# Recommender forward pass: 401 instead of 132 gathered tiles fetched row by row, other rings and buffers, and a reordered end

## The chip, the cores and the metric

The kernel runs on one core of a Trainium2 chip. The metric is the device time in microseconds (us) of one execution, the lower the better. Profiles show one execution; its span is the time from its first to its last instruction. The engines are named as in the profile: PE (TensorE, with PEld for its weight loads), DVE (VectorE), ACT (ScalarE), POOL (GpSimd) and SP (SyncE). PEq, ACTq, POOLq and SPq are their queues of instructions, in which DMAs are issued.

## The reference

The reference scores 16,384 samples. Each has 69 user fields and one label, all of them row numbers of one table `emb` of 100,001 rows with 96 numbers (384 bytes). Cut to what matters:

```python
u  = emb[batch_user]                      # 16384 x 69 x 96
ql = emb[batch_label[:, 0]]               # 16384 x 96
z  = concat([q, u, q - u, q * u])         # q is ql, once for each field
h  = dice(z @ W1 + b1, a1)                # 64 numbers
att = (h @ W2 + b2) @ W3 + b3             # one number for each field
pre = where(batch_user < ITEM_NUM, u * att, 0)
pooled = einsum('gf,bfe->bge', window, pre)     # 69 fields into 10 groups
x  = concat([pooled, ql])
h  = dice(bn(x @ Wf1 + bf1), af1)         # 200 numbers
h  = dice(bn(h @ Wf2 + bf2), af2)         # 80 numbers
return h @ Wf3 + bf3                      # one score for each sample
```

`dice(x)` is `(alpha * (1 - p) + p) * x` with a sigmoid `p` of `x`. In bytes, nearly all of the work is the fetching of 16,384 x 69 rows.

## The kernel before

The samples are cut into 32 blocks (`NBLK`) of 512. A **chunk** is one field of one block: 512 rows, in four tiles of 128 rows. There are 32 x 69 = 2208 chunks, and the main loop takes them in 1104 **pairs**, one pair in a step.

**Fetching.** `fetch(i)` (L354) fills one buffer of `upool` with the pair's eight tiles. For each tile POOL issues one indirect DMA (`gather`, L255, the instruction at L256), which fetches 128 rows by 128 row numbers in SBUF. PE turns each tile (`transpose`, recorded at L318) into `ptr`, features on partitions. DVE copies `ptr` to `uT` (L369) and multiplies it with the label's rows to `quT` (L370). The labels' own rows come by four gathers for each block (`head_gather`, L322). `upool` has 14 buffers, so POOL can be up to 14 pairs ahead of PE.

**Single rows.** The last tile (`SLOT` 3) of some chunks is not gathered. Its 128 rows are fetched by 128 direct DMAs of 384 bytes, issued by SP or ACT (`class Singles`, L268). For 32 rows at a time the queue reads 32 offsets from SBUF into registers (L279), and then it issues one DMA for each row (L294). The tile lands in a buffer of a ring (`ring`), four buffers for each of the two engines; PE waits on a semaphore for all 128 rows (`wait_for_single`, L311). SP issues a tile for one chunk in 17 steps (`SP_STEPS`), 64 in all, each a whole tile at once, placed in its queue 24 steps ahead of its use. ACT issues 8 rows in each step (`ACT_ROWS`), a tile in 16 steps, 68 in all; its rows stand between its activations, the first four ahead of the step's sigmoid and the others behind it in groups of three (`busy`, L506).

**Attention.** `hidden(i)` (L372) makes the hidden layer `ph` of a pair on PE (L377, L379), and ACT its sigmoid `y` (L381). `gate` (L384) is an activation on ACT (L386) and a product on DVE (L387). `attend` (L389) has one more matmul for each chunk (`pa`, L394), and DVE multiplies it with `uT` to `pre` (L396).

**Top.** `top1` (L398) adds the chunk's share of the 200 numbers to two sums `p` in PSUM (L407), in two halves of 100; a chunk is two matmuls in the code and four in the trace, as each of them runs as two passes. The last field closes the block: `top1_gates`, `top2`, `top3` and `store` make its scores.

**The order** is written out by hand: `plan` is a list of work for each step, filled by `at(step, ...)`, and every engine runs its instructions in this order. In step i of the main part stand the gate of pair i-3, `attend` of pair i-4, the hidden layer of pair i-2, `top1` of pair i-5 and the fetch of pair i. So a result of ACT is used a step after it was made. The last `CLOSE` = 6 steps (L551 to L579) have shorter distances: the hidden layer of the last pair, its `attend` and `top1`, and the whole top of the last block come after the last gather. In them ACT issues no rows. The functions of the change follow.

Of the kernel before, what the change touches and what calls it, by code (L numbers as in the profile page):

```python
# [18 lines left out]
P = 128  # L19
# [17 lines left out]

NUT, NQUT = 12, 8

CLOSE = 6  # L40

NV = 4
PER_BANK = 512 // F

ROW_BYTES = 4 * E
SLOT = 3
SP_STEPS = 17
SP_FIRST = 8
SP_AHEAD = 24
SP_CHUNKS = [2 * (int(SP_STEPS * s) + SP_FIRST) + 1 for s in range(64)]  # L50
SP_RING = 4
ACT_ROWS = 8
ACT_FIRST = 4
ACT_GROUP = 3
ACT_AHEAD = 5
ACT_CHUNKS = [2 * ((s + 1) * P // ACT_ROWS + ACT_AHEAD) for s in range(68)]
ACT_RING = 4
SINGLES = SP_CHUNKS + ACT_CHUNKS
NSB = (len(SINGLES) + P - 1) // P
NSEM = 4  # L60
RING_BYTES = 4096


# [51 lines left out]
def rec_kernel(  # L115
# [15 lines left out]

    const = ctx.enter_context(tc.tile_pool(name="const", bufs=1))
    ipool = ctx.enter_context(tc.tile_pool(name="ipool", bufs=2))
    upool = ctx.enter_context(tc.tile_pool(name="upool", bufs=14))
    ypool = ctx.enter_context(tc.tile_pool(name="ypool", bufs=4))
    ppool = ctx.enter_context(tc.tile_pool(name="ppool", bufs=6))
    bpool = ctx.enter_context(tc.tile_pool(name="bpool", bufs=2))
# [125 lines left out]
    def call(f, *args):  # L263
        return lambda: f(*args)
# [43 lines left out]
    def single(c, t):  # L308
        return places.get(c) if t == SLOT else None
# [41 lines left out]
            if k < m  # L351
        ]

    def fetch(i, between=None):  # L354

        u = upool.tile([P, 8, E], F32, tag="u", name=f"u{i}")
        for j in range(2):
            if j == 1 and between:
                between()
            c = 2 * i + j  # L360
            n, k = chunk_of(c)
            ptr = ps_tr.tile([E, BLK], F32, tag="tr", name=f"ptr{c}")
            for t in range(NQ):
                if single(c, t):
                    wait_for_single(c, t)
                else:
                    gather(rows, u[:, 4 * j + t, :], ids[n][:, 4 * k + t : 4 * k + t + 1])
                read_rows(nc.tensor.transpose, ptr[:, t * P : (t + 1) * P], u, c, t, ident)
            nc.vector.tensor_copy(uTs[c % NUT][0:E], ptr)  # L369
            nc.vector.tensor_tensor(quTs[c % NQUT][0:E], ptr, qTs[n % 2][0:E], ALU.mult)  # L370
# [27 lines left out]
    def top1(c):  # L398
# [6 lines left out]
        pre = pres.pop(c)  # L405
        for h, p in enumerate(p1s[n]):
            nc.tensor.matmul(p, V[:, k, h * DH : (h + 1) * DH], pre, start=False, stop=(k == F - 1))  # L407

    def top1_gates(n):

# [43 lines left out]
        nc.vector.tensor_copy(r, p4)  # L454
        nc.sync.dma_start(out=out[n0 * P : n1 * P].rearrange("(m p) o -> m (p o)", p=P), in_=r)

    def top3_last(n):
        x2 = x2s.pop(n)
        p3 = ps_x.tile([1, BLK], F32, tag="x", name="p3_last")
        nc.tensor.matmul(p3, wf3, x2, start=True, stop=True)  # L460
        r = ypool.tile([P, BLK], F32, tag="y", name="r_last")[0:1]
        nc.vector.tensor_scalar(r, p3, bf3c[0:1], None, ALU.add)
        nc.sync.dma_start(out=out[n * BLK :].rearrange("p o -> o p"), in_=r)

    pres, p1s, x1s, x2s, qs, phs, ys = ({} for _ in range(7))
# [3 lines left out]
    def at(step, *work):  # L469
        plan.setdefault(step, []).extend(work)  # L470
# [81 lines left out]
    tops(c, late + both(c - 5))  # L552
    at(c, call(attends, c - 3))
    tops(c, both(c - 4))
    at(c, call(fetch, c, call(hide, c - 1)))
    at(c + 1, call(attends, c - 2))
    tops(c + 1, both(c - 3))
    at(c + 1, call(attends, c - 1))
    tops(c + 1, both(c - 2))
    at(c + 1, call(fetch, c + 1, call(hide, c)))  # L560
    for i in range(c + 2, NPAIR):
        tops(i, both(i - 3))
        at(i, call(attends, i - 2), call(fetch, i, call(hide, i - 1)))
    i = NPAIR
    tops(i, both(i - 3))
    at(i, call(hide, last), call(attends, i - 2))
    tops(i, both(i - 2))
    at(i, call(store, 0, (NBLK - 1) * NQ), call(attends, last))
    tops(i, both(last))

    def finish():
        n = NBLK - 1
        for job in top1_gates(n):
            job()
        for job in top2(n):
            job()
        top3_last(n)

    at(i, finish)  # L579

    for n in range(NBLK):
        first = n * F // 2
# [86 lines left out]
```

## Time and profile before

| | |
|---|---|
| runs of the kernel before | 11,058.13, 11,061.62, 11,063.75 us (median 11,061.62) |
| the profiled execution: its own time | 11,063.24 us |
| its span | 11,061.5 us |
| PE busy | 9580.9 us, 87% of the span |
| POOL busy | 8332.4 us, 75% |
| DVE busy | 5087.8 us, 46% |
| ACT busy | 2055.4 us, 19% |
| mean clock granted to PE | 0.929 of full speed |
| moved by DMA | 456.87 MB, 41 GB/s |

A share of busy time alone does not tell the bound: PE's share grows where its clock is low, and the time in which ACT and SP issue DMAs is not counted as busy. In the rows of the groups, the numbers behind the bar are the busy time in us and the mean of one instruction in ns, then the idle time ahead of these instructions and what ended it. In a row of waits stand the sum in us, the number of times and the longest. A row of the timeline has its start and length in us, the engine, the line, and after x the number of instructions merged; in brackets the idle time before it. A row for one tile or line has the shortest, the median and the longest duration in ns, and the first and last start in us.

### The profile page before, as it was taken

What the parts mean: (1) busy time and instruction counts of PE and PEld (TensorE: products, weight loads), DVE (VectorE), ACT (ScalarE), POOL (GpSimd) and SP (SyncE); (2) the same over time, 40 slices, a digit from 0 to 9 for tenths busy, and PEclk for the clock granted to TensorE, in tenths of its full rate; (3) what the DMA queues carried; (4) which work ended last, traced back from release to release, by engine and by line L of the source; (5) the groups of instructions that cost most, each with busy time, mean ns of one, the idle gap of its engine ahead of it and who ended that gap; (6) DMA issues with size and microseconds to landing.
All of it is one profiled execution on the core that took longest, in us unless ns stands there. A gap on an engine that the chain in (4) does not pass through costs nothing.

```text
span 11061.5 us, 125036 instructions
## 1 busy us (share of the span) xinstructions
PE 9580.9 (87%) x32079; PEld 3517.5 (32%) x32079; DVE 5087.8 (46%) x7995; ACT 2055.4 (19%) x3058; POOL 8332.4 (75%) x8834
## 2 busy tenths in 40 slices
PE   8888888888888888888888888888888888888888
PEld 4333333333333333333333333333333333333333
DVE  4444444444444444444444444444444444444444
ACT  2211111111111111111111111111111111111111
POOL 7777777777777777777777777777777777777776
PEclk8999999999999999999999999999999999999999
DMA  2222222222222222222222222222222222222221
GB/s 55 41 42 42 41 41 41 43 41 41 41 41 43 41 41 41 41 43 41 41 41 41 43 41 41 41 41 43 41 41 41 41 43 41 41 41 41 40 40 35
DMA packets 319007, 456.87 MB, mean 41 GB/s; under 512 B 175253, under 2 KB 175889, under 8 KB 318162
## 3 DMA queue, kind: packets, MB, share of 16 engines
q0 software_dynamic: 282496, 434.48, 19.8%
q1 hardware_dynamic: 18386, 11.02, 0.4%
q10 hardware_dynamic: 17408, 3.38, 0.2%
q8 instruction: 259, 4.24, 0.2%
q14 instruction: 458, 3.75, 0.1%
HBM read 448.18 MB, written 0.07 MB: 41 GB/s over the span
## 4 chain that ended last, share of the span: by engine, by line
POOL 44%; PE 24%; issue 21%; DMA 10%; DVE 1%; ACT 0%; POOLq 0%; ACTq 0%; DVEq 0%
POOL u L256 43%; PE p L407 10%; DMA u<-in_rows,ids 10%; PE ph L377 4%; PE pa L394 4%; PE ph L379 3%; PE ptr L318 2%; POOL q L256 1%; PE pV L250 0%; PE p L404 0%; PE p L429 0%; DVE quT L370 0%; DMA q<-in_emb,ids 0%; DVE uT L369 0%; ACT g L437 0%
## 5 line engine op out<-in xcount | busy, mean ns | idle before, releaser
L256 POOL DMA_INDIRECT u<-in_rows,ids x8700 | 8210.8, 944 | 2652.6 <-issue 2481.3
L407 PE MATMUL p<-pre,V 96*100 96x512 f32 x8832 | 4077.9, 604 | 2.3 <-DVE pre L396 2.3
L369 DVE COPY uT<-ptr 96x512 f32<-96x512 f32 x2208 | 1512.1, 685 | 5307.5 <-PE ptr L318 5296.3
L318 PE MATMUL ptr<-ident,u 128*96 128x128 f32 x8700 | 1583.9, 286 | 1407.0 <-DMA u<-in_rows,ids 1380.6
L407 PEld LDWEIGHTS p<-pre,V 96*100 96x100 f32 x8832 | 1399.5, 168 | 2751.3 <-issue 2747.1
L381 ACT ACTIVATE y<-ph 128x512 f32<-128x512 f32 x1104 | 659.1, 597 | 7997.0 <-PE ph L379 7996.3
L318 PEld LDWEIGHTS ptr<-ident,u 128*96 128x96 f32 x8700 | 1030.2, 127 | 2461.4 <-DMA u<-in_rows,ids 1798.2
L396 DVE SCALAR_TENSOR_TENSOR pre<-pa,bb,uT 96x512 f32<-96x512 f32 x2208 | 1544.7, 738 | 43.1 <-PE pa L394 32.9
L394 PE MATMUL pa<-y,vrep 64*96 64x512 f32 x4416 | 1514.2, 723 | 43.8 <-DVE cT L342 18.4
L370 DVE TENSOR_TENSOR quT<-ptr,qT 96x512 f32<-96x512 f32 x2208 | 1492.9, 676 | 0.0
L377 PE MATMUL ph<-uT,AW 128*64 128x512 f32 x4416 | 1449.0, 737 | 0.9 <-ACT uT L349 0.9
L379 PE MATMUL ph<-quT,BW 128*64 128x512 f32 x4416 | 1291.1, 664 | 0.0
L386 ACT ACTIVATE y<-y,wn,na1c 128x512 f32<-128x512 f32 x1104 | 897.5, 813 | 604.2 <-ACT y L381 590.1
L387 DVE TENSOR_TENSOR y<-ph,y 128x512 f32<-128x512 f32 x1104 | 747.5, 677 | 22.7 <-ACT y L386 21.7
L379 PEld LDWEIGHTS ph<-quT,BW 128*64 128x64 f32 x4416 | 366.7, 159 | 816.2 <-issue 813.9
L377 PEld LDWEIGHTS ph<-uT,AW 128*64 128x64 f32 x4416 | 247.6, 153 | 1046.3 <-issue 998.5
L394 PEld LDWEIGHTS pa<-y,vrep 64*96 64x96 f32 x4416 | 324.5, 173 | 310.9 <-issue 90.4
L349 ACT COPY uT<-cT 32x512 f32<-32x512 f32 x384 | 230.1, 611 | 69.3 <-issue 50.6
L438 DVE SCALAR_TENSOR_TENSOR x<-p,wf,g 80x512 f32<-80x512 f32 x32 | 23.9, 746 | 304.1 <-ACT g L437 304.1
L349 ACT COPY quT<-cT 32x512 f32<-32x512 f32 x256 | 155.7, 608 | 1.1 <-DVE cT L342 1.1
L256 POOL DMA_INDIRECT q<-in_emb,ids x128 | 121.0, 945 | 40.7 <-issue 38.7
L420 DVE SCALAR_TENSOR_TENSOR x<-p,wf,g 100x512 f32<-100x512 f32 x64 | 46.6, 751 | 137.2 <-ACT g L419 137.2
(60 smaller groups left out, 731.5 us busy)
## 6 DMA issues: line engine op xcount, KB each, us to landing
ring<-in_rows ACTq DMA_DIRECT2D x8704, 0.4 KB
u<-in_rows,ids POOLq DMA_INDIRECT x8700
ring<-in_rows SPq DMA_DIRECT2D x8192, 0.4 KB
ids<-in_idx SPq DMA_DIRECT2D x8, 560.0 KB, 3.8
wv<-in_fields SPq DMA_DIRECT2D x1, 2434.5 KB, 12.1
q<-in_emb,ids POOLq DMA_INDIRECT x128
wn<-in_near SPq DMA_DIRECT2D x1, 226.0 KB, 3.2
wf<-in_far SPq DMA_DIRECT2D x1, 184.0 KB, 3.2
```

The costliest lines, as they stand in the source:

```text
L256: nc.gpsimd.indirect_dma_start(out=dst, out_offset=None, in_=table, in_offset=bass.IndirectOffsetOnAxis(ap=index, axis=0),)
L318: ins = op(out, ring[:, at[0]].bitcast(F32) if at else u[:, 4 * (c % 2) + t, :], other, **how)
L369: nc.vector.tensor_copy(uTs[c % NUT][0:E], ptr)
L370: nc.vector.tensor_tensor(quTs[c % NQUT][0:E], ptr, qTs[n % 2][0:E], ALU.mult)
L377: nc.tensor.matmul(p, AW, uTs[c % NUT], start=True, stop=False)
L379: nc.tensor.matmul(p, BW, quTs[c % NQUT], start=False, stop=True)
L381: nc.scalar.activation(y, ph, AF.Sigmoid, scale=S_DICE)
L386: nc.scalar.activation(ys[i], ys[i], AF.Identity, bias=a1c, scale=na1c)
L387: nc.vector.tensor_mul(ys[i], phs.pop(i), ys[i])
L394: nc.tensor.matmul(pa, vrep[at], ys[i][at], start=True, stop=True)
L396: nc.vector.scalar_tensor_tensor(pres[c], pa, bb[0:E], uTs[c % NUT][0:E], ALU.add, ALU.mult)
L407: nc.tensor.matmul(p, V[:, k, h * DH : (h + 1) * DH], pre, start=False, stop=(k == F - 1))
```

## The change

SP fetches 206 tiles row by row instead of 64 (one in 5.3 steps instead of 17, placed 14 steps ahead instead of 24), and ACT 195 instead of 68 (23 rows in a step instead of 8). Each of them has a ring of six buffers instead of four, with six semaphores. The buffers of pairs in `upool` go from 14 to 12.

The special end begins nine steps before the last instead of six. In its last four steps other work is put between the transposes of a fetch: the hidden layer of the pair before, the `top1` of two chunks, and an `attends`. After the last gather, `top1` of one chunk stands ahead of the last hidden layer and another behind it. The last two chunks' `top1` runs in two halves of 256 samples (`top1_last`), and the last block's top layers run in the same halves (`finish`), with one of each pair of gate activations on DVE instead of ACT. The store of the other 31 blocks' scores goes one step ahead, in front of the last hidden layer.

```diff
-CLOSE = 6
+CLOSE = 9
+HALVES = slice(0, BLK // 2), slice(BLK // 2, BLK)
...
-SP_STEPS = 17
+SP_STEPS = 5.3
 SP_FIRST = 8
-SP_AHEAD = 24
-SP_CHUNKS = [2 * (int(SP_STEPS * s) + SP_FIRST) + 1 for s in range(64)]
-SP_RING = 4
-ACT_ROWS = 8
+SP_AHEAD = 14
+SP_CHUNKS = [2 * (int(SP_STEPS * s) + SP_FIRST) + 1 for s in range(206)]
+SP_RING = 6
+ACT_ROWS = 23
...
-ACT_CHUNKS = [2 * ((s + 1) * P // ACT_ROWS + ACT_AHEAD) for s in range(68)]
-ACT_RING = 4
+ACT_CHUNKS = [2 * ((s + 1) * P // ACT_ROWS + ACT_AHEAD) for s in range(195)]
+ACT_RING = 6
...
-NSEM = 4
+NSEM = 6
...
-    upool = ctx.enter_context(tc.tile_pool(name="upool", bufs=14))
+    upool = ctx.enter_context(tc.tile_pool(name="upool", bufs=12))
...
-    def fetch(i, between=None):
+    def fetch(i, between={}):
         u = upool.tile([P, 8, E], F32, tag="u", name=f"u{i}")
         for j in range(2):
-            if j == 1 and between:
-                between()
...
             for t in range(NQ):
+                for work in between.get((j, t), ()):
+                    work()
                 if single(c, t):
...
+    def top1_last(n):
+        for s in HALVES:
+            for k in (F - 2, F - 1):
+                for h, p in enumerate(p1s[n]):
+                    weights = V[:, k, h * DH : (h + 1) * DH]
+                    nc.tensor.matmul(p[:, s], weights, pres[n * F + k][:, s], start=False, stop=(k == F - 1 and s is HALVES[1]))
...
+    def finish():
...
+        for s in HALVES:
+            for h in range(2):
+                nc.scalar.activation(
+                    g1[h][:, s], p1s[n][h][:, s], AF.Sigmoid, bias=dice1[h][0], scale=S_BN * S_DICE
+                )
+            nc.scalar.activation(g1[0][:, s], g1[0][:, s], AF.Identity, bias=dice1[0][1], scale=dice1[0][2])
+            nc.vector.tensor_scalar(g1[1][:, s], g1[1][:, s], dice1[1][2], dice1[1][1], ALU.mult, ALU.add)
+            for h in (1, 0):
+                nc.vector.scalar_tensor_tensor(
+                    x1[:, h, s], p1s[n][h][:, s], bf1c[h], g1[h][:, s], ALU.add, ALU.mult
+                )
+        for s, p in zip(HALVES, p2):
+            for h in (1, 0):
+                nc.tensor.matmul(p, wf2[:, h, :], x1[:, h, s], start=(h == 1), stop=(h == 0))
+            nc.scalar.activation(g2[:, s], p, AF.Sigmoid, bias=sb, scale=S_BN * S_DICE)
+            nc.vector.tensor_scalar(g2[:, s], g2[:, s], sna, sa, ALU.mult, ALU.add)
+            nc.vector.scalar_tensor_tensor(x2[:, s], p, bf2c, g2[:, s], ALU.add, ALU.mult)
+        for s, p in zip(HALVES, p3):
+            nc.tensor.matmul(p, wf3, x2[:, s], start=True, stop=True)
+            nc.vector.tensor_scalar(r[:, s], p, bf3c[0:1], None, ALU.add)
         nc.sync.dma_start(out=out[n * BLK :].rearrange("p o -> o p"), in_=r)
...
-    for i in range(c + 2, NPAIR):
+    for i in range(c + 2, c + 5):
         tops(i, both(i - 3))
-        at(i, call(attends, i - 2), call(fetch, i, call(hide, i - 1)))
-    i = NPAIR
+        at(i, call(attends, i - 2), call(fetch, i, {(1, 0): [call(hide, i - 1)]}))
+    i = c + 5
     tops(i, both(i - 3))
-    at(i, call(hide, last), call(attends, i - 2))
-    tops(i, both(i - 2))
-    at(i, call(store, 0, (NBLK - 1) * NQ), call(attends, last))
-    tops(i, both(last))
...
+    at(i, call(attends, i - 2))
+    for i in range(c + 5, NPAIR):
+        between = {
+            (0, 2): [call(hide, i - 1)],
+            (0, 3): [call(top1, 2 * i - 4)],
+            (1, 0): [call(top1, 2 * i - 3)],
+            (1, 2): [call(attends, i - 1)],
+        }
+        at(i, call(fetch, i, between))
+    at(last, call(store, 0, (NBLK - 1) * NQ))
+    at(NPAIR, call(top1, 2 * last - 2), call(hide, last), call(top1, 2 * last - 1))
+    at(NPAIR, call(attends, last), call(top1_last, NBLK - 1), finish)
```

More of the change, by code (lines that the diff above doesn't have):

```diff
@@ L455, in store @@
         nc.sync.dma_start(out=out[n0 * P : n1 * P].rearrange("(m p) o -> m (p o)", p=P), in_=r)
[L457 to L460, printed above, removed]
-        r = ypool.tile([P, BLK], F32, tag="y", name="r_last")[0:1]
-        nc.vector.tensor_scalar(r, p3, bf3c[0:1], None, ALU.add)
+    def finish():
+        n = NBLK - 1
+        x1 = xpool.tile([DH, 2, BLK], F32, tag="x1", name="x1_last")
+        g1 = [xpool.tile([DH, BLK], F32, tag=f"g{h}", name=f"g1_last_{h}") for h in range(2)]
+        x2 = xpool.tile([D2, BLK], F32, tag="x2", name="x2_last")
+        g2 = ypool.tile([P, BLK], F32, tag="y", name="g2_last")[0:D2]
+        r = ypool.tile([P, BLK], F32, tag="y", name="r_last")[0:1]
+        p2 = [ps_x.tile([D2, BLK // 2], F32, tag="x", name=f"p2_last_{k}") for k in range(2)]
+        p3 = [ps_h.tile([1, BLK // 2], F32, tag="h", name=f"p3_last_{k}") for k in range(2)]
+        sb, sa, sna = dice2
+        for s in HALVES:
[18 more added lines that the diff above has]
+            nc.vector.tensor_scalar(r[:, s], p, bf3c[0:1], None, ALU.add)
         nc.sync.dma_start(out=out[n * BLK :].rearrange("p o -> o p"), in_=r)
@@ L554, in rec_kernel @@
     tops(c, both(c - 4))
-    at(c, call(fetch, c, call(hide, c - 1)))
+    at(c, call(fetch, c, {(1, 0): [call(hide, c - 1)]}))
     at(c + 1, call(attends, c - 2))
@@ L559, in rec_kernel @@
     tops(c + 1, both(c - 2))
-    at(c + 1, call(fetch, c + 1, call(hide, c)))
-    for i in range(c + 2, NPAIR):
+    at(c + 1, call(fetch, c + 1, {(1, 0): [call(hide, c)]}))
+    for i in range(c + 2, c + 5):
         tops(i, both(i - 3))
-        at(i, call(attends, i - 2), call(fetch, i, call(hide, i - 1)))
-    i = NPAIR
+        at(i, call(attends, i - 2), call(fetch, i, {(1, 0): [call(hide, i - 1)]}))
+    i = c + 5
     tops(i, both(i - 3))
-    at(i, call(hide, last), call(attends, i - 2))
-    tops(i, both(i - 2))
-    at(i, call(store, 0, (NBLK - 1) * NQ), call(attends, last))
-    tops(i, both(last))
[L571 to L579, printed above, removed]
+    at(i, call(attends, i - 2))
[10 more added lines that the diff above has]
+    at(NPAIR, call(attends, last), call(top1_last, NBLK - 1), finish)
     for n in range(NBLK):
```

## The prediction

> **What bounds the kernel now.** I read the groups of instructions first, then who waits for whom on GpSimd (POOL), then the timeline at the first and at the last gather.
>
> ```profile
> L256 POOL DMA_INDIRECT u<-in_rows,ids x8700 | 8210.8, 944 | 2652.6 <-issue 2481.3
> L256 POOL DMA_INDIRECT q<-in_emb,ids x128 | 121.0, 945 | 40.7 <-issue 38.7
> POOL u L256 <- issue: 2481.3, 8138, 0.3
> POOL u L256 <- PE ptr L318: 76.2, 250, 0.3
> 3.27 1.10 POOL L256 DMA_INDIRECT q<-in_emb,ids  x1 [1.96 <-DMA ids<-in_idx]
> 11025.38 0.94 POOL L256 DMA_INDIRECT u<-in_rows,ids  x1 [0.30 <-issue]
> ```
>
> Busy and idle time of the two gather groups add up to 8210.8 + 2652.6 + 121.0 + 40.7 = 11,025.1 us. No wait in front of a gather is longer than 0.3 us, whoever it is put down to: POOL issues one gather after the other from 3.27 us to 11,025.38 us. With 8700 + 128 = 8828 gathers the pitch is (11,025.38 - 3.27) / 8827 = **1.2487 us**. A step (a pair of chunks) without single rows has 8 gathers, 9.99 us. The "75% busy" of POOL hides this, since the 0.30 us between gathers is not counted.
>
> TensorE (PE) looks busier, but its 87% stretches with the clock:
>
> ```profile
> 5000.98 2.03 PE L394 MATMUL pa<-y,vrep 64*96 64x512 f32 x4
> 5011.16 1.10 PE L394 MATMUL pa<-y,vrep 64*96 64x512 f32 x4
> 105.78 3.61 PE p L407 x8
> 113.16 3.61 PE p L407 x8
> ```
>
> The same four matmuls take 2.03 us in one step and 1.10 us in the next. While PE catches up after its late start (last two rows, from the chain of waits), a step takes 113.16 - 105.78 = 7.38 us. PE has room down to 7.38 us; POOL has none.
>
> **The change, part by part: the gathers.** A tile of 128 single rows replaces one gather. Before there are 64 + 68 = 132 such tiles, after 206 + 195 = 401, on distinct chunks. So 269 gathers go, and 8559 are left (8431 of rows, 128 of labels). 269 x 1.2487 = **335.9 us** off the last gather's start, which moves to 3.27 + 8558 x 1.2487 = 10,689.6 us. The mean step becomes 8559 x 1.2487 / 1104 = 9.68 us. All of this stands on POOL's own path, if the two issuers of single rows keep up.
>
> **SyncE.** It issues 26,368 rows instead of 8192.
>
> ```profile
> SPq L294 <- PE ptr L318: 6871.5, 59, 123.4
> 6.27 49.01 SPq L294 DMA_DIRECT2D ring<-in_rows  x128
> 55.33 0.37 SPq L146 DMA_DIRECT2D ids<-in_idx  x1
> 57.91 201.83 SPq L294 DMA_DIRECT2D ring<-in_rows  x512
> 440.92 48.72 SPq L294 DMA_DIRECT2D ring<-in_rows  x128
> 4680.81 49.41 SPq L294 DMA_DIRECT2D ring<-in_rows  x128
> ```
>
> SP waits for a free buffer for 6871.5 us of the span, so most of its time is free. Between 55.70 and 57.91 it reads the next 32 offsets, 2.21 us. Four tiles without a stop take (201.83 + 2.21) / 4 = 51.0 us each; single tiles later take 48.72 + 2.21 = 50.9 to 49.41 + 2.21 = 51.6 us. With more of ScalarE's rows beside it I take 51.3. The last of 206 tiles is then issued by 6.27 + 206 x 51.3 - 2.2 and some 4 us for the eight loads of indices: 10,576 us. It is used in step 1094, after which 9 steps of 8 gathers follow: 10,689.6 - 71 x 1.2487 = 10,601 us. The margin is 25 us in a whole run; at 51.6 the tile is 37 us late. PE then wins back 9 x (9.99 - 7.38) = 23 us, so the end slips by 14 us. Cost: 0 to 14 us, I take 3. Six buffers instead of four let SP run 6 x 5.3 = 32 steps ahead, so it no longer waits for PE.
>
> **ScalarE (ACT).** It issues 23 rows in a step instead of 8, in one queue with the sigmoids, the gates and the label copies.
>
> ```profile
> 39.17 2.34 ACTq L294 DMA_DIRECT2D ring<-in_rows  x8
> 5021.63 1.25 ACTq L294 DMA_DIRECT2D ring<-in_rows  x4
> 5031.49 1.13 ACTq L294 DMA_DIRECT2D ring<-in_rows  x4
> 5032.67 0.81 ACT L386 ACTIVATE y<-y,wn,na1c 128x512 f32<-128x512 f32 x1 [0.65 <-ACT y L381]
> 5035.12 1.36 ACTq L294 DMA_DIRECT2D ring<-in_rows  x4
> 5042.82 0.81 ACT L386 ACTIVATE y<-y,wn,na1c 128x512 f32<-128x512 f32 x1 [0.65 <-ACT y L381]
> 5042.89 1.12 ACTq L294 DMA_DIRECT2D ring<-in_rows  x4
> L294 ACTq DMA_DIRECT2D ring<-in_rows x36: 213/213/447, 5021.6 to 5067.7; - x36
> L294 SPq DMA_DIRECT2D ring<-in_rows x128: 227/228/272, 5018.6 to 5067.1; - x128
> L294 ACTq DMA_DIRECT2D ring<-in_rows x88: 213/213/448, 5081.2 to 5178.5; - x88
> ```
>
> Eight rows in 2.34 us with 0.213 us for the last make a pitch of (2.34 - 0.213) / 7 = 0.304 us. A row does not wait for the activation ahead of it: it follows 0.07 us after the gate's start (5042.82, 5042.89). Where 32 offsets have to be read first it comes 2.45 us after the gate (5032.67, 5035.12), and its group takes 1.36 instead of 1.13: 2.38 + 0.23 = 2.6 us for a reading, 23/32 of it in each step, 1.87 us. Two activations, 0.07 us in front of a row each, and the gaps around them make an estimated 0.25 us. So an ACT step is 23p + 2.12. At p = 0.304 that is 9.11 us. The worst group beside a busy SP (1.25 us for 4) gives p = 0.346 and 10.07 us. I take p = 0.314, **9.3 us**: the last three rows are ACT beside a busy SP, that SP tile, and ACT after it, and the medians do not move, 213 ns both times. 9.3 is under 9.68, so the cost is nothing. What hides it is the work of PE and the wait for gathers: an ACT that is late makes its gate late, behind it VectorE's product for PE's `pa`, which the code puts a step later. If that cover is gone, PE waits for ACT in each step and the 12 buffers of pairs fill.
>
> [...]
>
> **Twelve buffers of pairs instead of 14.** POOL is furthest ahead of PE at the start:
>
> ```profile
> L256 POOL DMA_INDIRECT u<-in_rows,ids x74: 940/944/962, 8.4 to 99.6; - x74
> L318 PE MATMUL ptr<-ident,u x40: 272/306/450, 20.0 to 93.5; 128*96 128x128 f32 x40
> ```
>
> By 100 us 74 tiles were gathered and 40 turned, a lead of 34, or 4.3 pairs. In the first four steps ACT also copies V for PE, and has 15 rows more ahead of these copies, 15 x 0.304 = 4.6 us each step, some 20 us or 16 gathers in all. Six to seven pairs are below 12, cost nothing; if the lead reached 12, each further gather would wait.
>
> **The last nine steps and the halves.** The tail before, from the last gather (11,025.38) to the end at 11,061.5, is 36.1 us:
>
> ```profile
> 11027.85 0.39 PE L318 MATMUL ptr<-ident,u 128*96 128x128 f32 x1 [0.86 <-DMA u<-in_rows,ids]
> 11028.03 5.26 PE L407 MATMUL p<-pre,V 96*100 96x512 f32 x8
> 11035.24 0.60 ACT L381 ACTIVATE y<-ph 128x512 f32<-128x512 f32 x1 [8.58 <-PE ph L379]
> 11036.72 0.69 DVE L387 TENSOR_TENSOR y<-ph,y 128x512 f32<-128x512 f32 x1 [7.15 <-ACT y L386]
> 11038.11 7.07 PE L407 MATMUL p<-pre,V 96*100 96x512 f32 x8 [1.92 <-DVE pre L396]
> 11045.23 1.55 PE L394 MATMUL pa<-y,vrep 64*96 64x512 f32 x4
> 11047.16 3.68 PE L407 MATMUL p<-pre,V 96*100 96x512 f32 x8 [0.39 <-DVE pre L396]
> 11059.27 0.24 SPq L463 DMA_DIRECT2D out<-r_last  x1
> ```
>
> After the last transpose two chunks of `p` (5.26 us) stood ahead of the last pair's `ph`; now one does, saving half, 2.6 us. Between that pair's sigmoid (11,035.24) and its `pa` (11,045.23) lay 9.99 us, most of it the next two chunks at 7.07 us; only the sigmoid, the gate and the product (to 11,037.41) have to be there, with one chunk beside them, at most 3.5 us: saving 6.5 to 7.8. `pa` to the last chunks' `p` stays 1.93 us, and these 3.68 us stay, as twice as many matmuls of half width. From their end (11,050.84) to the store (11,059.27) are 8.43 us of nine dependent operations and their gaps; at half width each is between half as long and unchanged, 4.2 to 8.4, I take 5.4: saving 3.0. Together 2.6 + 7.0 + 3.0 = 12.6 us. The tail becomes 23.5 us; bounds 20 (all savings high) and 30 (slow matmuls such as the 7.07 us group in place of 3.68, +3.4, and no gain from halves). The reordered work of the last steps has 9.99 us of gathers to hide behind; uncovered, one chunk is 1.8 us.
>
> **Sum.** 10,689.6 + 3 (SP) + 23.5 = 10,716 us of span; at 1.7 us around it (11,063.24 for a span of 11,061.5) the execution is 10,718. The profiled execution stands 1.6 us above the median of the runs. **I predict 10,718 us.** The main case reaches from 10,700 (tail 20, quiet issuers) to 10,760 (tail 30, SP at 51.6, late ACT).
>
> **Rivals.** *A: an issuer binds a little.* With ACT at a per step, PE leaves step 5 at some 125 us (105.78 plus the 20 above) and the end is 125 + 1080a + 19 x 7.38 + 24. This passes the forecast at a = 9.65, p = 0.327; at a = 9.8 it gives 10,873 us. For: the 1.25 us group. Against: the medians. SP alone does it above 51.55 us a tile, 206 us for each further us.
>
> *B: every gather slows.* If all took the slowest 962 ns instead of 944, 8559 x 0.018 = 154 us: 10,872. Against: the rows above hold for stretches with SP busy.
>
> *C: ACT's rows cost so much beside SP's that the kernel gets slower.* The place is the row's issue in ACT's queue. It decides from p = 0.341 (a = 9.975, the old span). At the 0.346 of the worst group, a = 10.07 and 125 + 10,876 + 140 + 24 = 11,165 us. For: one group of four; ACT's share of time beside SP rises from under a third (64 tiles of 51 us) to nearly all. Against: the 36 rows beside the busy SP, with the median of the others.
>
> *D: nothing moves,* since PE is bound after all: excluded down to 7.38 us a step, unless the slow clock stays on; near 11,061.
>
> *E: the two issuers take turns, row by row.* Then SP's 0.228 us and ACT's 0.213 us never overlap, and all rows need 26,368 x 0.228 + 24,960 x 0.213 = 11,328 us, slower than before. Against: beside the busy SP tile, whose 128 rows fill 29 of its 48 us, well over half of ACT's 36 rows would have waited, and their median would show it. [...]
>
> **Chances.** Main case 0.60, a tail or pitch below it 0.04, A 0.22, B 0.04, C 0.05, D 0.03, E 0.02. Range 10,698 to 10,880: the main case, B, and the larger part of A. This kernel's measurement can tell 0.2%, 22 us, from no change: faster 0.90, same 0.03, slower 0.07.
>
> **What would show it.** Right: 8559 gathers with a pitch near 1.249 us and no wait of POOL over 0.3 us; last gather at 10,690 to 10,700; SP without waits for `ptr`, its tiles at 51 to 51.6 us; sigmoids of `y` that still wait for `ph` for a part of each step; 20 to 30 us after the last gather. Wrong: POOL waiting for `ptr` (buffers full) for tens of us, PE waiting for `y` or its product (ACT binds), transposes of `ring` waiting for their rows (SP binds), rows of ACT at 0.33 us or more.

## The result, and the profile after

The changed kernel takes **11,227.1 us** (median; 11,222.93 to 11,232.92), the kernel before 11,062.26 us beside it: a ratio of 1.015 [1.0132, 1.0168]. It is slower, where 10,718 us was forecast. The profiled execution took 11,232.92 us, its span is 11,230.5 us, and its last gather starts at 11,202.25 us. A kernel's time is the median of its runs; one run of rows_768_bytes_again, 12,644.87 us at a granted clock of 0.68 instead of 0.92, is left out of its median.

All 269 gathers are gone, as counted. What moved is their pitch: (11,202.25 - 3.27) / 8558 = **1.3086 us** instead of 1.2487. 8558 x 0.0599 = 513 us are lost there, more than the 336 us won.

First the queues of DMAs and the chain of work that ended last, on the page of the kernel before, then on that of the changed kernel with its largest group. A row of a queue has its packets, MB and the time that its packets took, as a share of the sixteen DMA engines of the core. The profile counts what they moved in packets: in the records of the kernel before 141,248 of 3072 bytes for 8828 gathers, 16 for each, and one of 384 bytes for each single row, each of them with one more of 4 bytes.

```profile
q0 software_dynamic: 282496, 434.48, 19.8%
q1 hardware_dynamic: 18386, 11.02, 0.4%
q10 hardware_dynamic: 17408, 3.38, 0.2%
...
POOL 44%; PE 24%; issue 21%; DMA 10%; DVE 1%; ACT 0%; POOLq 0%; ACTq 0%; DVEq 0%
```

```profile
q0 software_dynamic: 273888, 421.24, 19.9%
q1 hardware_dynamic: 54738, 18.20, 2.8%
q10 hardware_dynamic: 49920, 9.68, 2.2%
...
DMA 37%; POOL 19%; PE 16%; ACTq 14%; issue 12%; DVE 1%; ACT 1%; POOLq 0%; DVEq 0%
...
L258 POOL DMA_INDIRECT u<-in_rows,ids x8431 | 7954.8, 944 | 3068.1 <-issue 2165.5
```

q0 carries the gathers, q1 SP's DMAs, q10 ACT's rows. A gather itself still takes POOL 944 ns; its idle time went from 2652.6 to 3068.1 us, though there are fewer gathers. The chain now runs through DMA for 37% instead of 10%. The two queues of single rows carry three times as many rows, but their share went from 0.6% to 5.0%, eight times as much. 5.0% of sixteen engines is 80% of one; with the 19.9% that the gathers' packets take on each engine, if they are spread evenly, it is 100% of one engine. This sum is a sign and no proof: two other kernels at the same limit give 104% and 86% (below). The chain also has ScalarE's queue (ACTq) for 14%, where it had 0%; whether that queue is the cause is rival Q of the experiments.

The waits in front of the gathers, in the table of waits of the changed kernel (sum in us, times, longest):

```profile
POOL u L258 <- issue: 2165.5, 6990, 2.5
...
POOL u L258 <- DMA u<-in_rows,ids: 687.0, 1097, 3.8
...
POOL u L258 <- PE ptr L320: 93.9, 148, 2.0
```

Before, no gather waited for longer than 0.3 us; now gathers wait for the landing of another gather for up to 3.8 us. The 93.9 us put down to PE's `ptr` are not full buffers: by the single records POOL is at most 42 tiles ahead of PE in this kernel, and 12 buffers hold 96. The busy time of POOL by stretches of the changed kernel, the number of gathers behind the x:

```profile
core 0: us, POOL busy (x), PEclk, DMA share, GB/s
0.00:1000.00 1000.00, 691.10 (x733) 0.91 0.25 43
1000.00:3000.00 2000.00, 1415.49 (x1501) 0.91 0.26 40
3000.00:5000.00 2000.00, 1451.76 (x1539) 0.92 0.26 41
5000.00:7000.00 2000.00, 1450.62 (x1539) 0.92 0.25 41
...
9000.00:10868.00 1868.00, 1362.10 (x1445) 0.92 0.26 41
10868.00:11202.00 334.00, 252.55 (x268) 0.95 0.19 41
```

2000 us hold 1602 gathers at a pitch of 1.2487 us; here they hold 1501 to 1539, from start to end. Only the last row is at full rate: 334 / 268 = 1.246 us. It begins where SP has issued its last row:

```profile
L296 SPq DMA_DIRECT2D ring<-in_rows x26368: 227/228/614, 7.4 to 10868.8; - x200
...
L296 ACTq DMA_DIRECT2D ring<-in_rows x24960: 213/214/586, 26.5 to 11038.6; - x200
```

This is the view of the line that issues the single rows. Their issue has medians of 228 and 214 ns, where 228 and 213 were. The wait table of SP's queue shows it idle at times, waiting for a free buffer:

```profile
SPq L296 <- PE ptr L320: 295.0, 68, 14.9
```

So SP's queue is not the bound. Worked out from the single records of the trace, not from a view: the gathers use eight semaphores in turn, and each waits for the gather eight before it, 9.99 us at full pitch. A gather lands in 16 parts, each of which adds one to the semaphore: the records of the changed kernel have 136,115 landings on the eight semaphores, 15.9 for each of 8559 gathers. Medians, from the gather's start:

```
us to landing of             15th part    16th part   90th percentile of the 16th
kernel before                  2.46         2.50         2.61
changed kernel                 2.49         8.46        10.79
```

Fifteen parts come as before, one comes 6 us late. 1005 gathers start more than 0.04 us late and lose 510 us together; 971 of them, with 481 us, start within 0.8 us after the landing of the gather eight before, the median of the late ones 0.26 us after it, and no gather of the run starts sooner than that.

The tail, in the timeline (rows left out):

```profile
11202.25 0.94 POOL L258 DMA_INDIRECT u<-in_rows,ids  x1 [0.30 <-issue]
...
11206.55 0.42 PE L320 MATMUL ptr<-ident,u 128*96 128x128 f32 x2
...
11211.44 0.60 ACT L383 ACTIVATE y<-ph 128x512 f32<-128x512 f32 x1 [8.35 <-PE ph L381]
...
11213.66 1.10 PE L396 MATMUL pa<-y,vrep 64*96 64x512 f32 x4 [0.40 <-DVE y L389]
...
11215.60 3.70 PE L417 MATMUL p<-pre,V 96*100 96x256 f32 x16 [0.83 <-DVE pre L398]
...
11223.12 2.00 PE L491 MATMUL p_last<-x_last,wf 100*80 100x256 f32 x4 [1.05 <-DVE x_last L486]
...
11225.05 1.01 PE L496 MATMUL p_last<-x_last,wf 80*1 80x256 f32 x2
...
11226.73 1.01 PE L496 MATMUL p_last<-x_last,wf 80*1 80x256 f32 x2 [0.67 <-DVE x_last L494]
...
11228.28 0.24 SPq L498 DMA_DIRECT2D out<-r_last  x1
```

From the last gather to the end are 28.2 us, against 36.1 before and 23.5 forecast.

### The profile page after: what moved, and what is told of

Read it like the earlier page. It is cut to its first block, busy times and chain, and to the rows that moved or that the text cites. A ratio compares the mean times of both kernels' runs of the same rounds, so it can differ in the third digit from the quotient of the medians.

```text
span 11230.5 us, 194874 instructions
## 1 busy us (share of the span) xinstructions
PE 9751.0 (87%) x32093; PEld 3607.3 (32%) x32093; DVE 5092.2 (45%) x8003; ACT 2097.6 (19%) x3060; POOL 8076.4 (72%) x8565
## 3 DMA queue, kind: packets, MB, share of 16 engines
q0 software_dynamic: 273888, 421.24, 19.9%
q10 hardware_dynamic: 49920, 9.68, 2.2%
## 4 chain that ended last, share of the span: by engine, by line
DMA 37%; POOL 19%; PE 16%; ACTq 14%; issue 12%; DVE 1%; ACT 1%; POOLq 0%; DVEq 0%
DMA u<-in_rows,ids 36%; POOL u L258 19%; ACTq L296 11%; PE p L409 5%; ACTq L281 3%; PE pa L396 3%; PE ph L379 3%; PE ph L381 2%; PE ptr L320 1%; DMA q<-in_emb,ids 1%; ACT y L388 0%; PE p L406 0%; PE pV L252 0%; PE p L439 0%; DVE pre L398 0%
## 5 line engine op out<-in xcount | busy, mean ns | idle before, releaser
L258 POOL DMA_INDIRECT u<-in_rows,ids x8431 | 7954.8, 944 | 3068.1 <-issue 2165.5
L320 PE MATMUL ptr<-ident,u 128*96 128x128 f32 x8431 | 1417.9, 283 | 1007.4 <-DMA u<-in_rows,ids 989.2
L396 PE MATMUL pa<-y,vrep 64*96 64x512 f32 x4416 | 1674.6, 719 | 360.8 <-DVE pre L398 281.7
L320 PEld LDWEIGHTS ptr<-ident,u 128*96 128x96 f32 x8431 | 991.8, 127 | 1912.0 <-DMA u<-in_rows,ids 1224.1
L379 PE MATMUL ph<-uT,AW 128*64 128x512 f32 x4416 | 1526.7, 752 | 72.7 <-ACT uT L351 72.2
L381 PE MATMUL ph<-quT,BW 128*64 128x512 f32 x4416 | 1377.4, 683 | 0.0
L396 PEld LDWEIGHTS pa<-y,vrep 64*96 64x96 f32 x4416 | 388.1, 173 | 761.1 <-DVE pre L398 440.5
```

The costliest lines, as they stand in the source:

```text
L258: nc.gpsimd.indirect_dma_start(out=dst, out_offset=None, in_=table, in_offset=bass.IndirectOffsetOnAxis(ap=index, axis=0),)
L320: ins = op(out, ring[:, at[0]].bitcast(F32) if at else u[:, 4 * (c % 2) + t, :], other, **how)
L379: nc.tensor.matmul(p, AW, uTs[c % NUT], start=True, stop=False)
L381: nc.tensor.matmul(p, BW, quTs[c % NQUT], start=False, stop=True)
L396: nc.tensor.matmul(pa, vrep[at], ys[i][at], start=True, stop=True)
```

## The experiments

The theory, **S**: every single row runs on the same one of the sixteen DMA engines, whoever issues it. At some 4.6 rows a microsecond beside the gathers that engine is full; the part of each gather that runs on it comes late, and POOL stops at the gather eight later. Its rivals: **Q**, that ScalarE's 23 rows in a step do it, in ScalarE's own queue; **B**, the 12 buffers of pairs; and the price of a row by its bytes rather than by its DMA. By S the sum of both issuers' rows decides, by Q ScalarE's alone.

All edits are made to the changed kernel. Eight kernels (sp206_act68, sp64_act195, end_only, bufs14, sp206_act136, sp206_act161, sp149_act195 and rows_768_bytes) ran in two sets, on chips 0 and 15, in which the kernel before itself takes 13,345 and 13,249 us; they are called the first sets here. All but end_only were run once more where it takes 11,062 to 11,084 us, under the same name with "again". It is not a matter of the chip's number: on chip 15 the kernel before takes 11,062 us in a later set. What was different in the first sets is not known.

**One issuer at a time.** SyncE's 206 tiles with ScalarE's 68 of before (35,072 rows), and ScalarE's 195 with SyncE's 64 (33,152 rows):

```diff
-ACT_ROWS = 23
+ACT_ROWS = 8
-ACT_CHUNKS = [2 * ((s + 1) * P // ACT_ROWS + ACT_AHEAD) for s in range(195)]
+ACT_CHUNKS = [2 * ((s + 1) * P // ACT_ROWS + ACT_AHEAD) for s in range(68)]
```

```diff
-SP_STEPS = 5.3
+SP_STEPS = 17
-SP_AHEAD = 14
-SP_CHUNKS = [2 * (int(SP_STEPS * s) + SP_FIRST) + 1 for s in range(206)]
+SP_AHEAD = 24
+SP_CHUNKS = [2 * (int(SP_STEPS * s) + SP_FIRST) + 1 for s in range(64)]
```

> The changed kernel with ScalarE back at 8 rows a step (68 tiles); SyncE keeps 206. Theory S (all single rows go through one of the 16 DMA engines, which is full; each gather's share on it lands late, and a gather waits for the one eight before it): 35,072 rows instead of 51,328. At the changed kernel's 0.175 us of that engine a row (80% of 11,202 us for 51,328 rows) they need 56% of it beside the 20% of the gathers, so it isn't full, the gathers keep their pitch of 1.249 us, and 8686 of them end at 10,849 us; with the tail of 28 us the time is 10,878. Theory Q (ScalarE's queue with 23 rows a step is what holds everything up): the same 10,878, as ScalarE is relieved. Theory B (12 buffers instead of 14 are too few): near 11,227.

> The changed kernel with SyncE back at 64 tiles in 17 steps; ScalarE keeps 195 tiles, 23 rows a step. Theory S: 33,152 rows, 52% of the one DMA engine beside 20%: not full, 8701 gathers at 1.249 us end at 10,867 us, time 10,897. Theory Q: ScalarE has as much to do in each step as in the changed kernel, so the step stays at 10.1 us and the time near 11,227. Theory B: near 11,227.

Measured: 17,328 us (ratio 1.300 [1.2952, 1.3056]) and 14,953 us (1.1215). These times do not bear on the cause looked for. In the first sets the queues that issue the rows are the bound, as the chain of waits and SP's timeline of sp206_act68 show:

```profile
SPq 64%; issue 36%; PE 1%; DVE 0%; DMA 0%; ACT 0%; DVEq 0%
```

```profile
4999.99 198.88 SPq L296 DMA_DIRECT2D ring<-in_rows  x282
```

282 rows in 199 us; the same kernel run once more (sp206_act68_again) issues 499 in that time:

```profile
5000.01 199.92 SPq L296 DMA_DIRECT2D ring<-in_rows  x499
```

The median of a row's issue is 228 ns in both, but in the first sets a quarter of the rows come 0.73 us or more after the one ahead, where it is 3% in sp206_act68_again. It is another bound than that of the changed kernel at 11,227 us, and says nothing on S or Q. So both were run again:

> The changed kernel with ScalarE back at 8 rows a step, once more: in the first set the kernel before itself took 13,345 us, as every queue of instructions stood still again and again for about 0.7 us, and no gather waited for an earlier one. Where the kernel before takes 11,062 us, theory S (one DMA engine carries all single rows and is full in the changed kernel): 35,072 rows fill 56% of it beside 20% for the gathers, the 8686 gathers keep 1.249 us, 10,878. Theory Q (ScalarE's 23 rows a step hold it up): 10,878 too.

> The changed kernel with SyncE back at 64 tiles, ScalarE at 23 rows a step, once more. Where the kernel before takes 11,062 us, theory S: 33,152 rows, the engine is not full, 8701 gathers at 1.249 us, 10,897. Theory Q: ScalarE has as much to do as in the changed kernel, near 11,227.

Measured: sp206_act68_again **10,880.24 us**, ratio 0.9835 [0.9819, 0.9851], 2 us from the count of gathers. SyncE's part of the change alone is a gain, at a pitch of 1.249 us, and POOL's waits for landings are back at 0.3 us:

```profile
POOL u L258 <- issue: 2413.5, 7909, 0.3
...
POOL u L258 <- DMA u<-in_rows,ids: 97.9, 321, 0.3
```

sp64_act195_again: **10,935.41 us**, 0.9885 [0.9868, 0.9901]. With all 23 of ScalarE's rows in each step it is faster than before too: Q, which expected 11,227, falls. It misses S's count (10,897) by 38 us. The stretches say where:

```profile
core 0: us, POOL busy (x), PEclk, DMA share, GB/s
0.00:1000.00 1000.00, 724.96 (x768) 0.93 0.23 45
1000.00:5000.00 4000.00, 3022.88 (x3203) 0.93 0.20 42
```

33 gathers are missing in the first 1000 us, where SP issues its first tiles without a pause, beside ScalarE (by the single records the two issue 4.8 to 5.0 rows a microsecond between 100 and 400 us, and 3.1 from 1000 us on); later 4000 / 3203 = 1.249 us. So the rate of the moment counts, and not only the mean, on which S's count was based.

**The end alone.** The new order of the end and the halves, with both issuers, rings and buffers as before:

```diff
 (both edits above, and)
-SP_RING = 6
+SP_RING = 4
-ACT_RING = 6
+ACT_RING = 4
-NSEM = 6
+NSEM = 4
-    upool = ctx.enter_context(tc.tile_pool(name="upool", bufs=12))
+    upool = ctx.enter_context(tc.tile_pool(name="upool", bufs=14))
```

> The kernel before with only the reordered last nine steps and the halves: single rows, rings and 14 buffers as before. Theories S and Q: the gathers are untouched, and only the tail behind the last gather shrinks, from 36.1 to the 28.2 us of the changed kernel: 11,054, 8 us under the kernel before. If the reordering itself cost time in the last steps, it would be 11,062 or more.

Measured: 13,343.7 us against 13,344.85, ratio 0.9997 [0.9987, 1.0008]. Eight microseconds of 13,345 are 0.06%, inside that interval: inconclusive, and it was not run again. The tail is seen better in the profiles: 28.2 us in the changed kernel and 28.1 in sp206_act68_again, where no gather is late.

**14 buffers.**

```diff
-    upool = ctx.enter_context(tc.tile_pool(name="upool", bufs=12))
+    upool = ctx.enter_context(tc.tile_pool(name="upool", bufs=14))
```

> The changed kernel with 14 buffers of pairs instead of 12. Theory B: the waits of the gathers go, 10,720. Theories S and Q: GpSimd is about one pair ahead of TensorE in the changed kernel, so no buffer is missing and the time stays at 11,227.

> The changed kernel with 14 buffers of pairs instead of 12, where the kernel before takes 11,062 us. Theory B (12 buffers are too few): the waits of the gathers go, 10,720. Theory S (one full DMA engine): GpSimd is about one pair ahead of TensorE in the changed kernel, no buffer is missing, 11,227 as with 12.

Measured: 16,851 us (1.264) in the first sets, where the issue of rows is the bound; then **11,229.71 us**, 1.0131 [1.0114, 1.0148], an interval that overlaps that of the changed kernel. The loaded engine is as it was (changed kernel: 2.8%, 2.2%):

```profile
q1 hardware_dynamic: 54738, 18.20, 2.8%
q10 hardware_dynamic: 49920, 9.68, 2.3%
```

B falls. By the records of the changed kernel POOL's lead over PE is a median of 10 tiles (a pair has 8) and at most 42, so 12 buffers are never full.

**The dose.** By S rows can be added at 1.2487 us gained for each 128, until the engine is full; from there each row costs its time on the engine. SyncE stays at 206 tiles, ScalarE goes up; one kernel has the same sum in another mix:

```diff
-ACT_ROWS = 23
+ACT_ROWS = 16      (19, 20, 21)
-... for s in range(195)]
+... for s in range(136)]      (161, 169, 178)
```

```diff
-SP_STEPS = 5.3
+SP_STEPS = 7.3
-SP_CHUNKS = [2 * (int(SP_STEPS * s) + SP_FIRST) + 1 for s in range(206)]
+SP_CHUNKS = [2 * (int(SP_STEPS * s) + SP_FIRST) + 1 for s in range(149)]
```

> The changed kernel with 16 rows of ScalarE a step, 136 tiles, beside SyncE's 206. Theory S (one DMA engine for all single rows): 43,776 rows at 0.175 us are 71% of it beside 20%: not yet full. 8618 gathers at 1.249 us and the tail of 28 us: 10,796. Theory Q (ScalarE's queue): ScalarE's step is about 7 us, no hindrance, 10,796.

> The changed kernel with 19 rows of ScalarE a step, 161 tiles. Theory S: 46,976 rows at 0.175 us are 76% of the engine beside 20%, 96%: at the edge. Without a wait 8593 gathers give 10,765; with landings that grow I expect 10,765 to 10,900, gathers that wait for the one eight before, and the 16th part of a gather late where the 15th is not. Theory Q: 10,765.

> The changed kernel with SyncE at 149 tiles (one in 7.3 steps); ScalarE keeps 195, 23 rows a step. In all 44,032 rows, as many as with 206 and 136 tiles. Theory S: only the sum of rows counts, so as fast as that kernel: 8616 gathers, 10,794, with up to 40 us more from the first 250 us, where SyncE issues without a stop and fills the engine. Theory Q: ScalarE's queue is as full as in the changed kernel, near 11,227.

Measured: 17,086.86 us (1.289), 17,061.23 (1.288) and 14,856.72 (1.120) against 13,248.99: the first sets once more, and again nothing on S.

> Once more, as in that set the kernel before took 13,249 us. 206 tiles by SyncE and 136 by ScalarE. Where the kernel before takes 11,062 us, theory S: 43,776 rows are 71% of the one DMA engine beside 20%, not yet full; 8618 gathers at 1.249 us and the tail of 28 us, 10,796. Theory Q: 10,796 too.

> 19 rows of ScalarE a step, 161 tiles, beside SyncE's 206, where the kernel before takes 11,062 us. Theory S: 46,976 rows at 0.175 us are 76% of the one DMA engine beside 20%, at the edge: without a wait 8593 gathers give 10,765, with growing landings 10,765 to 10,900. Theory Q (ScalarE's queue): 10,765.

> 149 tiles by SyncE, 195 by ScalarE (23 rows a step), where the kernel before takes 11,062 us. Theory S: only the sum of rows counts, 44,032, as many as with 206 and 136 tiles, which took 10,795: 10,794, with up to 40 us more from the first 250 us, where SyncE issues without a stop. Theory Q: ScalarE's queue is as full as in the changed kernel, near 11,227.

> 20 rows of ScalarE a step, 169 tiles, beside SyncE's 206. Theory S: 48,000 rows at 0.175 us are 78% of the one DMA engine beside 20%: 98%, the last step before it is full. 8585 gathers at 1.249 us and the tail of 28 us give 10,755 without a wait; the kernel with 161 tiles was 6 us above its count, so 10,755 to 10,800.

> 21 rows of ScalarE a step, 178 tiles, beside SyncE's 206. Theory S: 49,152 rows at 0.175 us are 80% of the one DMA engine beside 20%: full at the pace of 10,744 us that 8576 gathers would have. Some gathers wait for the one eight before; slower than with 169 tiles, 10,760 to 11,000. If nothing is full at this sum, 10,744.

Measured, each against the kernel before beside it (11,061.8 to 11,062.9 us); the landing of the 16th part is from the records of the traces:

```
                     rows   rows a us   median us of    late starts of
                           (to the last  the 16th part  gathers, us in all   us         ratio
                             gather)
kernel before       16896     1.53         2.50             0.2          11,062
sp64_act195_again   33152     3.04         2.51              38          10,935.41  0.9885 [0.9868, 0.9901]
sp206_act68_again   35072     3.23         2.50             0.2          10,880.24  0.9835 [0.9819, 0.9851]
sp206_act136_again  43776     4.07         2.62             0.2          10,795.48  0.9759 [0.9742, 0.9775]
sp149_act195_again  44032     4.07         3.64              58          10,850.36  0.9808 [0.9791, 0.9824]
sp206_act161_again  46976     4.37         3.26             5.6          10,771.02  0.9737 [0.9720, 0.9753]
sp206_act169        48000     4.47         3.81             9.4          10,765.60  0.9732 [0.9715, 0.9748]
sp206_act178        49152     4.58         6.73              27          10,769.97  0.9735 [0.9719, 0.9752]
changed kernel      51328     4.58         8.46             510          11,227.1   1.0150 [1.0132, 1.0168]
```

The mean stops at 4.58 rows a microsecond. The changed kernel would have needed 4.80 for the forecast time and got 4.58, bufs14_again the same and rows_768_bytes_again 4.57. sp206_act178 also has 4.58, but that is nearly all it asked for (49,152 rows in 8576 gathers of 1.2487 us are 4.59): it stands at the limit, not beyond it. These means hold the slower start and the ends; between 1000 and 10,500 us, by the single records, sp206_act178 issues 4.66 rows a microsecond at full pitch, and the changed kernel 4.67 to 4.73 with its gathers held back. By the mean, each row beyond the limit costs 1 / 4.58 = 0.218 us. 51,328 - 49,152 = 2176 rows would cost 475 us; the last gather comes 461.5 us later, and the times differ by 457 us. That is the jump from the fastest kernels to one slower than before, with 17 tiles. sp206_act136_again came within 1 us of its count (10,796).

The queues on the pages of sp206_act169, then of sp206_act178, with the waits of the latter behind:

```profile
q1 hardware_dynamic: 54738, 18.14, 1.7%
q10 hardware_dynamic: 43264, 8.39, 1.2%
```

```profile
q0 software_dynamic: 274432, 422.08, 20.6%
q1 hardware_dynamic: 54738, 18.14, 3.0%
q10 hardware_dynamic: 45568, 8.84, 2.2%
```

```profile
POOL u L258 <- issue: 2413.4, 7901, 0.6
...
POOL u L258 <- DMA u<-in_rows,ids: 119.4, 324, 2.2
```

In sp206_act178 the packets of single rows already take 16 x 5.2 = 83% of one engine, with the gathers' 20.6% a sum of 104%, and a gather's last part is late by 4 us in the median; but POOL waits only where it comes near the eight pitches of 9.99 us, and the 90th percentile is 8.34 us. So it costs 27 us, nearly all at the start, where 1580 gathers stand in 2000 us, and 1602 later:

```profile
0.00:2000.00 2000.00, 1490.97 (x1580) 0.92 0.26 44
2000.00:4000.00 2000.00, 1510.53 (x1602) 0.93 0.26 43
```

sp149_act195_again missed S's count (10,794, up to 40 us more) by 16 us. Its loss lies at the start too, 752 gathers in the first 1000 us where 801 fit:

```profile
0.00:1000.00 1000.00, 709.44 (x752) 0.92 0.25 44
1000.00:5000.00 4000.00, 3022.35 (x3203) 0.94 0.22 42
```

It also speaks against Q: with all of ScalarE's rows in it, and ACTq with a larger share of the chain than in the changed kernel, it runs at full pitch from 1000 us on.

```profile
POOL 28%; PE 21%; ACTq 20%; issue 17%; DMA 11%; ACT 1%; DVE 1%; POOLq 0%; DVEq 0%
```

The sum of rows is not all that counts, though: at the same rate of rows the 16th part lands later than in sp206_act136_again in the quiet part as well (3.63 against 2.62 us from 3000 us on). It costs nothing there; why the mix matters is not shown.

**By the DMA or by the byte.** Rows of 768 bytes instead of 384, of which only the first half is used; ring and table are made to fit:

```diff
-in_=row_bytes[:, bass.ds(self.values[r], ROW_BYTES)]
+in_=row_bytes[:, bass.ds(self.values[r], 2 * ROW_BYTES)]
```

> The changed kernel with single rows of 768 bytes instead of 384: each DMA also brings the next row of the table, which nobody reads. Theory S with a price for each DMA: the same time as the changed kernel, 11,227. Theory S with a price for each byte: the single rows take twice as long on the one engine, 51,328 x 0.35 us = 17,960 us. Theory Q: 11,227.

> Once more, for the same reason. The changed kernel with single rows of 768 bytes, of which 384 are used. Where the kernel before takes 11,062 us: theory S with a price for each DMA, 11,227 as the changed kernel; with a price for each byte, up to 17,960; theory Q, 11,227.

Measured: 16,743.99 us (1.268) in the first sets, then **11,258.5 us**, 1.0177 [1.0156, 1.0197]: with twice the bytes hardly more than the changed kernel.

```profile
q1 hardware_dynamic: 54738, 28.33, 2.2%
q10 hardware_dynamic: 49920, 19.27, 1.9%
```

The packets' share is even smaller (4.1% against 5.0%), and the 16th part lands at a median of 8.55 us. So between 384 and 768 bytes the price is one of the DMA, not of its bytes. With the gathers' 20.1% the sum for one engine is 86% here, at the same limit of 4.57 rows a microsecond: the packets' times do not measure how full the engine is, the rate at which it stops does.

**A row on two engines.** The row in two pieces of 192 bytes, from a table in which they stand 256 bytes apart:

```diff
-out=ring[r : r + 1, b], in_=row_bytes[:, bass.ds(self.values[r], ROW_BYTES)]
+out=ring[r : r + 1, b].rearrange("p (k n) -> p k n", k=2),
+in_=row_bytes[:, bass.ds(self.values[r], 512)].rearrange("p (k n) -> p k n", k=2)[:, :, 0 : ROW_BYTES // 2]
```

> The changed kernel, its single rows read from a second copy of the table in which a row lies as two halves of 192 bytes, 256 apart, so that each row's DMA has two pieces. Theory S says that a row's DMA runs on one DMA engine because it is one piece: with two pieces it should run on two, and of the 16 parts of a gather two should land late instead of one. The price was the same for 768 bytes as for 384, so each of the two engines should be as full as the one was: 11,227 or more. If halves cost half as much, the engines are not full and the time is near 10,720. If one engine carried both pieces, it would have twice the work: near 18,000.

Measured: **21,636.22 us**, 1.9556. None of the three expected times came. As a test of the time it is lost, since the issue of such a row is dearer: a median of 0.73 us from row to row instead of 0.32 and 0.30, so that the issuers bind. At 2.4 rows a microsecond nothing is full, and no part of a gather is late (the 16th at 2.49 us), so the two late parts that were expected could not show:

```profile
q1 hardware_dynamic: 107474, 18.31, 0.5%
q10 hardware_dynamic: 99840, 9.78, 0.3%
...
SPq 69%; ACTq 17%; issue 12%; PE 1%; ACT 0%; DVE 0%; another core or an unknown queue 0%; DMA 0%; POOL 0%; DVEq 0%
```

But its packets tell how a row is spread. Counted in the records of the traces, with the median time of a packet:

```
                          data packets               packets of 4 bytes
changed kernel, gathers   3072 bytes x136944, 214 ns   x136944   16 + 16 for each of 8559 gathers
changed kernel, SP rows    384 bytes x26368,  175 ns   x26581    1 + 1 for each row
changed kernel, ACT rows   384 bytes x24960,  173 ns   x24960    1 + 1
two parts, ACT rows        192 bytes x49920,   13 ns   x49920    2 + 2
kernel before, ACT rows    384 bytes x8704,    22 ns   x8704     1 + 1
```

A gather has one packet of 4 bytes for each of its 16 parts, a row one, a row in two pieces two. That fits one engine for a row and two for a row in two pieces; and packets of the same queue overlap in time in 1103 of 51,328 rows of the changed kernel, but 39,396 times in as many rows of two pieces. It is also one engine for both issuers, and not one for each: SP's and ACT's packets taken together overlap in 3991 of the 51,328 rows, though they fill some 80% of the time, and with two engines full a gather would have two late parts, where the 15th is on time. Whether two pieces would lift the bound stays open: it needs an issue that costs no more.

## Why the prediction was wrong

**The step that failed** is the end of the gathers' part: "All of this stands on POOL's own path, if the two issuers of single rows keep up." They kept up, and POOL did not. The prediction priced a single row where it is issued, in the queues of SP and ACT, and nowhere on the engine that carries it. The count of gathers was right, 8559, and so was the price of one where nothing is late: sp206_act68_again and sp206_act136_again hit their counts. But the pitch held only up to a mean of 4.58 rows a microsecond, and the change asked for 51,328 / 10,690 = 4.80. Instead one DMA engine, by the packets and the one late part, carried every single row beside a sixteenth of each gather; that sixteenth came late, and POOL, waiting for it eight gathers later, went to a pitch of 1.3086 us, 513 us in all. None of the rivals had this in it, so the range was too narrow on that side.

Put together from the profiled execution: 10,718 forecast, + 512.6 by the pitch (8558 x 0.0599), - 3 for SP, which was not late, + 4.7 in the tail, + 0.7 around the span = 11,233.0 us, against 11,232.92.

That it is one engine is worked out, not read: the records carry a row as one packet of 384 bytes and one of 4 bytes, a row in two pieces as two of 192 and two of 4, and one of a gather's 16 parts is late (8.46 us) where the 15th is on time (2.49 us); the engine's index is in no row here.

The profile of the kernel before would not have given the size: 0.6% of sixteen engines is 10% of one, and three times that is 30%. A packet of a row took 22 ns before and 175 ns after. That the limit comes at 4.58 rows was only to be had by adding rows.

**The bound.** Right: POOL's gathers are the bound of the kernel before, and a gather taken away is worth its pitch as long as the one engine is not full: in sp206_act136_again 210 fewer gathers bring the last one from 11,025.4 to 10,766.2 us, 1.23 us each. PE's matmuls did stretch with the clock: in the kernel before the four that took 2.03 us (at 5000.98) had a granted clock of 0.50, the four that took 1.10 us (at 5011.16) one of 1.00.

**SyncE.** Right: the medians of a row's issue did not move (228 ns), and the mean from row to row is 325 ns before and after. It was never late for its tiles; it waited for PE for 295 us, where no such wait was forecast. In sp206_act136_again, at the forecast pitch, that wait is 4.1 us in all and SP's last row starts at 10,579.9 us, where 10,576 was forecast for the end of its last tile.

**ScalarE.** Right in that it did not bind, with less room than was given: p, the mean from row to row inside a group, is 0.324 us by the single records (median 0.304), where 0.314 was taken, which makes a step of 23 x 0.324 + 2.12 = 9.57 us instead of 9.3, against 9.68. That ScalarE would hold 9.68 is not shown, as the changed kernel's steps took 10.1 us; sp149_act195_again, with the same 23 rows, holds 9.74. Rivals A and C, which let the issuers bind, are not what happened; in the first sets an issuer does bind, for another reason. **E**, that the two issuers take turns, row by row, is not borne out: with both engines issuing all the time the medians are 228 and 214 ns, and at these medians all rows one after the other would need 11,353 us, more than the 11,039 us in which they were issued.

**B, every gather slows.** The pitch of the gathers did grow, as B has it, but by accident: their own time stays at 944 ns, and the loss is 513 us, three times the 154 us given there.

**Twelve buffers.** Right, cost nothing: 14 give 1.0131 against 1.0150, with intervals that overlap.

**The tail.** Direction right, size off: 7.9 us won, not 12.6. The order did its part: from the last pair's sigmoid (11,211.44) to its `pa` (11,213.66) are 2.22 us instead of 9.99, a saving of 7.8 us, at the high end of what was given. The last transpose stands 4.3 us after the last gather, where it was 2.5, since PE has an `attends` and a chunk's `top1` in between: 1.8 us of the 2.6 expected there were given back. The halves saved nothing behind `p`: from its end (11,215.60 + 3.70) to the store (11,228.28) are 9.0 us, where 8.43 were and 5.4 were expected. PE's matmuls between the steps take up to 2.00 and 1.01 us there at half the width, as long as the 1.94 and 1.02 us that they took at full width, and there are twice as many operations. The width is not all of it: those of the changed kernel ran at a granted clock of 0.50, which began 8.7 us before the end of the span, while the kernel before had 1.00 up to its last 2.8 us; at 0.87 the same four matmuls of the first half (at 11,220.90) took 1.18 us. Seven more kernels with the new end show this drop too, 7.7 to 9.4 us before their end. What the halves would win at the full clock is not shown. So the term of the halves was mis-sized, from a gain of 3.0 us to a loss of 0.6, within the bounds given for the tail.

**What would show it wrong.** The list named waits of POOL for `ptr`, of PE for `y`, and late rows. It had the general sign, "no wait of POOL over 0.3 us", and that is the row which failed, with 3.8 us; the cause behind it was not on the list.

## What to carry to other kernels

A single row had a price where it was issued, 228 ns in SP's queue before and after, and another one on the engine that carried it, 0.218 us for each row beyond the limit. Before moving work to many small DMAs, ask on how many of the sixteen engines each of them runs, and multiply a queue's share by sixteen where it is one. Do not scale that share up from a light load: three times the rows took eight times the share here. Near the limit the time did not bend but broke: 17 tiles more, on 384, turned a gain of 2.7% into a loss of 1.5%, so such a change is tried in steps, and the landing of a gather's last part (2.5, 3.8, 6.7, 8.5 us) showed the limit before the time did. The fastest version run is sp206_act169, with 48,000 single rows: 10,765.60 us, 0.9732 [0.9715, 0.9748]; its neighbours with 161 and 178 tiles are within 6 us, and the intervals do not tell the three apart.

## What the runs showed of the hardware that was not expected

- The median packet of a row takes 22 ns in the kernel before and still 22 ns with 48,000 rows (sp206_act169), but 175 ns in sp206_act178 and in the changed kernel, though the row is the same. At the limit 4.58 rows a microsecond and 0.76 gathers fill an engine whose packets took 10% + 20% of it before. What the engine does in that time isn't shown by the runs; 768 bytes cost hardly more than 384 (11,258.5 against 11,227.1 us).
- Fifteen parts of a gather are not touched by the sixteenth: 2.44 and 2.49 us for the 14th and the 15th with the one engine full, 2.43 and 2.46 before.
- A late part cost next to nothing where the gather landed before its semaphore was used again, eight pitches (9.99 us) after its start: in sp206_act178 half of the gathers land at 6.73 us or later instead of 2.50, and POOL loses 27 us.
- A row in two pieces cost an issuing engine 0.73 us (rows_in_two_parts), more than twice the 0.32 and 0.30 us of a row in one piece.
- In the first sets a row's issue has the same median (228 ns), but 282 instead of 499 rows fit in 200 us, and the changed kernel with 14 buffers is 26% slower there than the kernel before.
